# Two message-passing layers on one core: the second layer sums its messages one unit later, makes its edge weights from halves of the partitions, and takes more rows by products

## The chip, the core and the metric

The kernel runs on one core of a Trainium2 chip. A core has five engines that run side by side, each with its own queue of instructions: TensorE (PE in the profile, with PEld for its weight loads), VectorE (DVE), ScalarE (ACT), GpSimd (POOL) and SyncE (SP), which here only starts transfers. The metric is the device time of one execution in microseconds (us). Three timed runs of the kernel before gave 5934.48, 5959.10 and 5971.08 us. One further execution was recorded by the profiler.

## The reference

There are 6250 nodes with 128 features and 200000 edges sorted by destination. Both layers normalise the node features, clip them at zero, send something along each edge, sum it at the destination and add the result to the features.

```python
h = relu(layernorm(x))
z = (h @ W).reshape(N, 8, 16)                       # layer 0: attention over edges
e = leaky_relu(el[src] + er[dst], 0.2)              # el, er: products of z with attn_l, attn_r
a = exp(e - segment_max(e, dst)[dst])
x = x + segment_sum(z[src] * a, dst) / segment_sum(a, dst) + bias

h = relu(layernorm(x))                              # layer 1: products of features and edge data
s, v = h[:, :32] @ W_up_s, einsum(h[:, 32:], W_up_v)
w0, w1, w2, w3 = split(silu(silu(edge8 @ A1 + b1) @ A2 + b2) @ A3, 4)     # weights of each edge
mji = concat(s[src]*y_s*w0, dot(v[src], y_v)/sqrt(3)*w3, s[src]*y_v*w1, v[src]*y_s*w2)
message = segment_sum(mji, dst) / 10
x = x + concat(ms @ W_out_s, mv @ W_out_v)
```

So each layer needs, for each of the 200000 edges, one row of a table of 6250 rows: the row of the edge's source node.

## The kernel before

Edges are laid out in 1563 tiles of 128 (one edge per partition), and 16 tiles make a block: `KB` = 16, `NB` = 98 blocks. Since edges are sorted by destination, a block touches a window of 128 nodes. Sums are made by TensorE: a tile of one-hot rows (`one_hot`, line 1170) times the tile of messages, accumulated over the block in one PSUM bank `p_u`.

**Rows by source.** A tile's 128 source rows are fetched in one of three ways.
- An indirect transfer issued by GpSimd (`gather`, line 836, issued in line 839): one instruction for each tile.
- Row by row from SyncE (`rows_by_row`, line 1141, issued in line 1154): 128 transfers of one row each, for the last tile of each third block.
- By products on TensorE, for tile `KD` = 14 of the blocks named in the sets `dense` (layer 0, line 1200) and `dense1` (layer 1, line 1201). The whole table lies in SBUF as three bf16 parts (`t0s`, `t1s`), a one-hot matrix of the sources is made by VectorE (`ends_to`, `dense_ends`), and 17 groups of 3 products pick the rows (`rows_of` line 1304, `dense_rows` line 1911).

The gathers of a block are issued in `take_rows`, three blocks ahead in layer 0 and two ahead in layer 1, into five buffers that go round.

**The start.** GpSimd gathers the raw features of the first `KX` = 25 tiles while the first table is being made (`gather_x`, line 903); those rows are normalised and multiplied like the table itself. The remaining tiles of block 1 come from the finished table `t0`. Five of the normalising steps of the table run on GpSimd (line 960). A count then decides between this path for evenly spread edges and a general one (line 1005); the profiled execution took this path.

**Layer 0** loops over blocks in an order written out by hand for TensorE, VectorE, ScalarE and SyncE. `asked` (line 1262) loads three tiles of the first table, `split` (line 1277) splits them into the bf16 parts, once per block.

**Between the layers** the last `NL` = 3 tiles of nodes aren't ready when the first gathers of layer 1 could start. The first `NE` = 24 tiles are gathered early, from a copy of the table `t1z` with zeros in those nodes, and what is missing is added by products (`late_ends`, `late_rows`).

**Layer 1** loops over units of four tiles (391 of them), in this order on TensorE: half a step of the edge network of the next block (`network`, line 1755, bank `p_h`, two of them), the edge weights of the next unit (`tensor_weights`, line 1780, two products of 256 columns over 128 partitions, for two tiles each; bank `p_w`, two of them), products for rows (`dense_step`), and the sums of this unit (`sums1`, line 1819, bank `p_u`, two of them), for which it waits for this unit's messages (`messages`, line 1794, on VectorE). A finished block is taken out by `finish` (line 1178), a finished tile of nodes is put out by `node1` (line 1831), whose bank is a part of `held`. `edge_rows` (line 1747) loads the edge data two blocks ahead.

Of the kernel before, what the change touches and what calls it, by code (L numbers as in the profile page):

```python
# [9 lines left out]
F32 = mybir.dt.float32  # L10
# [3 lines left out]
OP = mybir.AluOpType  # L14
# [4 lines left out]
P = 128  # L19
# [5 lines left out]
MU = 32  # L25
# [716 lines left out]
def tile_even_edges(  # L742
# [63 lines left out]
    KX = KB + 9  # L806
# [49 lines left out]
    with tc.manual_schedule(engines={mybir.EngineType.PE, mybir.EngineType.DVE,  # L856
# [81 lines left out]
        def rows_of(gx, xs, fp, fp_ps, raw=None):  # L938
# [5 lines left out]
            for k in range(NC + 3):  # L944
# [3 lines left out]
                if 0 <= c < NC:  # L948
# [3 lines left out]
                    for j in range(n):  # L952
# [4 lines left out]
                        else:  # L957
                            late = by in (0, 3, 5) and NC - 4 <= c < NC - 2 and not raw
                            eng = nc.gpsimd if late else nc.vector
                            eng.tensor_scalar(h[:, j, :], xs[c][:, j, :], mvs[c][:, j, 0:1],  # L960
                                              rs[:, j, :], op0=OP.subtract, op1=OP.mult)
# [49 lines left out]
def even_edges(tc, v):  # L1011
# [8 lines left out]
    with ExitStack() as ctx:  # L1020
# [28 lines left out]
        NL, NE = 3, 24  # L1049
# [83 lines left out]
        nc.sync.dma_start(a1p, v["a1p"])  # L1133
# [44 lines left out]
        def finish(b, p_u, width, carry, agg, pool):  # L1178
# [8 lines left out]
            carry = pool.tile([WB, MW], F32, name="carry")  # L1187
            nc.scalar.copy(carry[:, :width], p_u[WB:, :width])
            return carry, agg
# [10 lines left out]
        dense = set(range(-(-NX // TS) + 4, NB - 4))  # L1200
        dense1 = set(range(10, NB - 4, 4))
# [36 lines left out]
        with tc.manual_schedule(engines=in_order), \  # L1238
# [338 lines left out]
            for g in range(NG - 3):  # L1577
# [7 lines left out]
                asked(g - 2)  # L1585
# [29 lines left out]
                if was:  # L1615
                    rows_of(n1, half + 4, NR)
                if b4:
                    weights(b4)
# [4 lines left out]
                er_of(n1, 1)  # L1623
                turned(n1, 2)
# [9 lines left out]
                if to:  # L1634
                    rows_of(n2, 0, 3)
# [21 lines left out]
                split(g - 3)  # L1657
# [77 lines left out]
        with tc.manual_schedule(engines=in_order), \  # L1735
# [11 lines left out]
            def edge_rows(b):  # L1747
                if b < NB:
                    c = blk[b]
                    c["ft"] = l1.tile([P, P], F32, name="ft", bufs=4)  # L1750
                    nc.sync.dma_start(c["ft"], f8[:, b, :])
                    c["yb"] = l1.tile([P, KB, 4], F32, name="yb", bufs=4)
                    nc.sync.dma_start(c["yb"], y4[:, b * KB : (b + 1) * KB, :])

            def network(b, step):

# [10 lines left out]
                p_h = l1_ps.tile([P, 4, P], F32, name="p_h")  # L1767
# [12 lines left out]
            def tensor_weights(u):  # L1780
# [3 lines left out]
                w = u["w"] = l1_ps.tile([P, 4, 4, MU], F32, name="p_w")  # L1784
                for k in range(0, m, 2):
                    q, n = (k0 + k) // 2, min(2, m - k)
                    nc.tensor.matmul(w[:, k : k + n].rearrange("p k a u -> p (k a u)"),  # L1787
                                     c["h2"][q // 4][:, q % 4, :],
                                     a3p[:, :n].rearrange("p k f -> p (k f)"), start=True, stop=True)
# [29 lines left out]
            def sums1(u):  # L1819
                b, k0, m = u["b"], u["k0"], u["m"]  # L1820
                if k0 == 0:
                    blk[b]["p_u"] = l1_ps.tile([P, 512], F32, name="p_u")
# [342 lines left out]
```

## Time and profile before

| | |
|---|---|
| median of 3 timed runs | 5959.1 us |
| the profiled execution's own time | 3749.37 us |
| its span, first to last instruction | 3747.6 us |
| what lies around the span | 1.8 us |
| granted TensorE clock, mean | 0.936 |
| busy: PE, DVE, ACT, POOL | 85%, 70%, 38%, 75% |
| gathers in the span (1750 + 589 + 583 from tables, 24 from `t1z`, 25 raw) | 2971 |
| row transfers by SyncE | 7808 |

The profiled execution is 2209.7 us shorter than the median of the timed runs. The profile shows one execution only, and nothing in it tells where the timed runs spend the difference. "Busy" counts the time in which an engine has an instruction in it; TensorE's records overlap and their ends are modelled, so the start-to-start distance of its groups tells its pace better. Starting a transfer on SyncE isn't counted as busy.

### The profile page before, as it was taken

Reading aid. Unit: us, or ns where it says so; the run is one execution under the profiler, and the core shown is the slowest. Engines: PE = TensorE matmul, PEld = TensorE weight load, DVE = VectorE, ACT = ScalarE, POOL = GpSimd, SP = SyncE. Lnnn points to the kernel's source line nnn. Section 1 sums busy time; section 2 is a strip of 40 time slices with the busy share of each in tenths; the row PEclk is TensorE's granted clock in tenths of the full one; section 3 lists DMA queues with packets and bytes.
Section 4 is the critical chain, followed back from the end, with each engine's and each line's share of the span. In section 5 each row is a group of like instructions: output and inputs, shape, how many; then the busy total and the mean of one; then the engine's idle time right before and its main releaser. Section 6 shows DMA issues by size and latency. Waiting matters only on the chain. (4 is left out here: it accounts for less than half of the span.)

```text
span 3747.6 us, 74803 instructions
## 1 busy us (share of the span) xinstructions
PE 3196.4 (85%) x19845; PEld 2474.1 (66%) x19845; DVE 2633.1 (70%) x6272; ACT 1406.0 (38%) x3638; POOL 2817.3 (75%) x2981
## 2 busy tenths in 40 slices
PE   4756788888888888888788899999999999999997
PEld 4655566666666666666666677777677777767775
DVE  7755666666666666666657777777777777777776
ACT  4432333333333333333334444444444444444443
POOL 7777777777777777777777777777777777777776
PEclk7766899999999999999799999999999999999999
DMA  6333332222222222222223222222222222222222
GB/s 167 75 78 79 71 68 67 68 69 68 68 68 68 68 68 67 69 69 67 71 70 95 69 64 64 64 64 64 64 64 64 65 63 64 65 63 64 63 68 52
DMA packets 212534, 262.78 MB, mean 70 GB/s; under 512 B 77425, under 2 KB 163921, under 8 KB 212097
## 3 DMA queue, kind: packets, MB, share of 16 engines
q0 software_dynamic: 95072, 200.78, 22.6%
q1 hardware_dynamic: 116592, 57.03, 5.7%
q8 instruction: 159, 2.61, 0.3%
q14 instruction: 279, 2.28, 0.2%
q10 hardware_dynamic: 432, 0.09, 0.0%
HBM read 236.19 MB, written 21.14 MB: 69 GB/s over the span
## 5 line engine op out<-in xcount | busy, mean ns | idle before, releaser
L839 POOL DMA_INDIRECT fz<-ft,fsrc x1750 | 1654.1, 945 | 539.5 <-issue 327.0
L1824 PE MATMUL p_u<-mj,s 128*128 128x256 f32 x3126 | 764.3, 388 | 87.5 <-DVE mj L1816 86.5
L1313 PE MATMUL p_x<-t0s,fz_first 128*128 128x408 bf16 (+1 forms) x3723 | 730.0, 346 | 0.0
L1824 PEld LDWEIGHTS p_u<-mj,s 128*128 128x128 f32 x3126 | 582.2, 192 | 215.6 <-DVE mj L1816 139.7
L839 POOL DMA_INDIRECT fz_other<-ft,fsrc x589 | 557.2, 946 | 179.6 <-issue 107.6
L839 POOL DMA_INDIRECT fz_second<-ft,fsrc x583 | 554.0, 950 | 178.3 <-issue 107.9
L1313 PEld LDWEIGHTS <-fz_first 128*128 128x128 bf16 x3723 | 361.5, 101 | 231.5 <-issue 17.4
L1791 ACT ACTIVATE p_w<-p_w,yb 128x64 f32<-128x64 f32 x1563 | 451.5, 289 | 117.3 <-PE p_w L1787 73.8
L1787 PE MATMUL p_w<-fa3p,h 128*128 128x256 f32 x1564 | 408.4, 384 | 0.0
L1787 PEld LDWEIGHTS p_w<-fa3p,h 128*128 128x128 f32 x1564 | 286.7, 193 | 114.5 <-issue 48.8
L1772 ACT ACTIVATE h<-p_h,fb 128x512 f32<-128x512 f32 x196 | 134.7, 687 | 585.8 <-PE p_h L1770 575.1
L1337 ACT COPY mk<-p_m 128x384 f32<-128x384 f32 (+1 forms) x99 | 47.4, 479 | 658.5 <-PE p_m L1333 651.6
L1427 PE MATMUL p_u<-fz,s 128*128 128x136 f32 x1846 | 272.9, 308 | 20.1 <-DVE fz L1422 20.1
L1427 PEld LDWEIGHTS p_u<-fz,s 128*128 128x128 f32 x1846 | 258.5, 216 | 23.8 <-DVE fz L1422 22.2
L1173 DVE TENSOR_TENSOR s<-p_i,fdloc 128x512 f32<-128x512 f32 x391 | 268.6, 687 | 3.8 <-ACT p_i L1766 3.8
L1173 DVE TENSOR_TENSOR s<-p_m,fdloc 128x512 f32<-128x512 f32 x391 | 266.2, 682 | 3.0 <-ACT mk L1337 2.7
L1770 PE MATMUL p_h<-ft,fa1p 128*128 128x128 f32 x1568 | 216.1, 282 | 56.5 <-DMA ft<-in_e_f_dram 56.3
L1770 PEld LDWEIGHTS p_h<-ft,fa1p 128*128 128x128 f32 x1568 | 208.7, 197 | 79.8 <-issue 55.7
L1348 ACT CAST d<-p_d 128x512 bf16<-128x512 f32 x391 | 229.3, 586 | 78.0 <-PE p_d L1346 34.2
L1378 DVE TENSOR_TENSOR_SCAN pe<-mk,pe 128x128 f32<-128x128 f32 x98 | 42.0, 428 | 290.8 <-PE pe L1293 271.6
L1777 ACT ACTIVATE h<-p_h,fb 128x512 f32<-128x512 f32 x196 | 134.7, 687 | 260.4 <-PE p_h L1774 260.4
L1811 DVE TENSOR_REDUCE vd<-vy 128x128 f32<-128x384 f32 x391 | 229.6, 587 | 0.0
(285 smaller groups left out, 4880.5 us busy)
## 6 DMA issues: line engine op xcount, KB each, us to landing
r<-ft SPq DMA_DIRECT2D x3968, 0.5 KB
r<-ft SPq DMA_DIRECT2D x3840, 0.5 KB
fz<-ft,fsrc POOLq DMA_INDIRECT x1750
fz_other<-ft,fsrc POOLq DMA_INDIRECT x589
fz_second<-ft,fsrc POOLq DMA_INDIRECT x583
fx<-x SPq DMA_DIRECT2D x47, 160.0 KB
ft<-in_e_f_dram SPq DMA_DIRECT2D x98, 64.0 KB
t1s<-fx SPq DMA_DIRECT2D x7, 576.0 KB
```

The lines of the kernel that those rows point to most:

```text
L839: nc.gpsimd.indirect_dma_start(out=to[:, k, :width], out_offset=None, in_=table, in_offset=bass.IndirectOffsetOnAxis(ap=src_col[:, t : t + ...
L1173: nc.vector.tensor_tensor(s[:, :m], iota[:, None, :].to_broadcast([P, m, P]), dloc[:, t : t + m].unsqueeze(2).to_broadcast([P, m, P]), OP. ...
L1313: nc.tensor.matmul(c["p_x"][:, :m, :], c["oh", k // half][:, k % half, :], t0s[:, i::NR, s, :], start=k == 0 and s == 0, stop=k == NR - 1 ...
L1348: nc.scalar.copy(d[:, :m], p_d[:, :m])
L1427: nc.tensor.matmul(c["p_u"][:, :ZW], c["s"][k // 4][:, k % 4, :], c["z"][:, k, :], start=c["o"] + k == 0, stop=c["o"] + k == KT[c["b"]] - 1)
L1770: nc.tensor.matmul(p_h[:, q, :], a1p[:, q0 + q, :], c["ft"], start=True, stop=True)
L1772: nc.scalar.activation(c["h1"], p_h, AF.Silu, bias=b1)
L1777: nc.scalar.activation(h2, p_h, AF.Silu, bias=b2)
L1787: nc.tensor.matmul(w[:, k : k + n].rearrange("p k a u -> p (k a u)"), c["h2"][q // 4][:, q % 4, :], a3p[:, :n].rearrange("p k f -> p (k f) ...
L1791: nc.scalar.activation(w[:, k, ::2, :], w[:, k, ::2, :], AF.Copy, scale=c["yb"][:, k0 + k, 0:1])
L1811: nc.vector.tensor_reduce(vd, vy.rearrange("p t i u -> p t u i"), AX.X, OP.add)
L1824: nc.tensor.matmul(blk[b]["p_u"][:, :MW], u["s"][:, k, :], u["mj"][:, k, :], start=k0 + k == 0, stop=k0 + k == KT[b] - 1)
```

## The change

- In the start, `KX` grows from 25 to 29, and the five normalising steps on GpSimd go to VectorE.
- In layer 0, `dense` begins with block 12 and not 21; `asked` and `split` are called twice per block, for numbers 2g - 4 and 2g - 3 in block g, and not once for g - 2 and g - 3. `rows_of`, `turned` and `er_of` move within the step of a block.
- Between the layers, `NE` grows from 24 to 28.
- In layer 1, `dense1` takes three of eight blocks and not one of four. Counted out, that is 32 blocks for 21; in layer 0 it is 82 for 73.
- `sums1` runs one unit later, after the next unit's weights, and `finish` with the copy of the carry after that (`block_ended`).
- `tensor_weights` makes each tile's weights by its own product of 128 columns over 64 partitions, low and high half in turn, in another order of `a1p`; `p_w` takes two banks for each of its two buffers.
- `p_h` and `p_u` have one bank each for two; `node1` and `late_ends` use the bank of the network.
- `edge_rows` runs three blocks ahead with five buffers; the very last unit is cut in two.

```diff
-    KX = KB + 9
+    KX = KB + 13
...
-                            late = by in (0, 3, 5) and NC - 4 <= c < NC - 2 and not raw
-                            eng = nc.gpsimd if late else nc.vector
-                            eng.tensor_scalar(h[:, j, :], xs[c][:, j, :], mvs[c][:, j, 0:1],
-                                              rs[:, j, :], op0=OP.subtract, op1=OP.mult)
+                            nc.vector.tensor_scalar(h[:, j, :], xs[c][:, j, :], mvs[c][:, j, 0:1],
+                                                    rs[:, j, :], op0=OP.subtract, op1=OP.mult)
...
-        NL, NE = 3, 24
+        NL, NE = 3, 28
...
-        nc.sync.dma_start(a1p, v["a1p"])
+        halves = [a.rearrange("p (u k) (q f) -> p u k q f", k=2, q=2) for a in (a1p, v["a1p"])]
+        for k in range(2):
+            for q in range(2):
+                nc.sync.dma_start(halves[0][:, :, q, k, :], halves[1][:, :, k, q, :])
...
-        dense = set(range(-(-NX // TS) + 4, NB - 4))
-        dense1 = set(range(10, NB - 4, 4))
+        dense = set(range(-(-NX // TS // 2) + 3, NB - 4))
+        dense1 = {b for b in range(10, NB - 4) if b % 8 in (2, 4, 7)}
...
-                asked(g - 2)
+                for k in range(2):
+                    asked(2 * g - 4 + k)
...
-                split(g - 3)
+                for k in range(2):
+                    split(2 * g - 4 + k)
...
-                p_h = l1_ps.tile([P, 4, P], F32, name="p_h")
+                p_h = l1_ps.tile([P, 4, P], F32, name="p_h", bufs=1)
...
-                w = u["w"] = l1_ps.tile([P, 4, 4, MU], F32, name="p_w")
-                for k in range(0, m, 2):
-                    q, n = (k0 + k) // 2, min(2, m - k)
-                    nc.tensor.matmul(w[:, k : k + n].rearrange("p k a u -> p (k a u)"),
-                                     c["h2"][q // 4][:, q % 4, :],
-                                     a3p[:, :n].rearrange("p k f -> p (k f)"), start=True, stop=True)
+                p_w = l1_ps.tile([P, 4, 2 * P], F32, name="p_w")
+                w = u["w"] = p_w[:, :, :P].rearrange("p k (a u) -> p k a u", u=MU)
+                for t in sorted(range(k0, k0 + m), key=lambda t: t % 2):
+                    q, half_t = t // 4 * 2 + t % 2, t // 2 % 2
+                    on = slice(64 * half_t, 64 * half_t + 64)
+                    nc.tensor.matmul(p_w[:, t - k0, :P], c["h2"][q // 4][on, q % 4, :], a3p[on, half_t],
+                                     start=True, stop=True)
...
-                    blk[b]["p_u"] = l1_ps.tile([P, 512], F32, name="p_u")
+                    blk[b]["p_u"] = l1_ps.tile([P, 512], F32, name="p_u", bufs=1)
...
+                p_n = l1_ps.tile([P, 4, P], F32, name="p_h", bufs=1)[:, :2]
...
+            def block_ended():
+                nonlocal carry, agg, ends
+                if ends is not None:
+                    p_u, to_carry = blk[ends]["p_u"], l1n.tile([WB, MW], F32, name="carry")
+                    nc.scalar.copy(to_carry, p_u[WB:, :MW])
+                    agg = finish(ends, p_u, MW, carry, agg, l1n)
+                    carry = to_carry
+                    if ends % 2 == 1:
+                        done.append((ends // 2, agg))
+                    ends = None
...
                 late_ends(4 * (i + 2))
+                if i:
+                    ends = sums1(us[i - 1])
                 messages(u)
...
-                sums1(u)
-                if k0 + m == KT[b]:
-                    ends = b
```

## The prediction

> **What bounds the kernel now.** I read the page's first part, then the busy times by stage, then GpSimd's timeline, then TensorE's within one unit. In the first line TensorE looks like the bound.
>
> ```profile
> PE 3196.4 (85%) x19845; PEld 2474.1 (66%) x19845; DVE 2633.1 (70%) x6272; ACT 1406.0 (38%) x3638; POOL 2817.3 (75%) x2981
> ```
>
> The stages speak otherwise. One stretch of layer 0, one of layer 1 (columns: length, then PE, PEld, DVE, ACT, POOL with counts, clock, DMA):
>
> ```profile
> 1499.20:1686.60 187.40, 165.97 (x1297) 122.35 (x1295) 126.71 (x265) 58.46 (x134) 141.91 (x150) 0.95 0.30 69
> 3185.80:3373.20 187.40, 170.83 (x842) 132.32 (x843) 141.21 (x349) 81.62 (x229) 141.66 (x151) 0.99 0.25 64
> ```
>
> The layers differ in work, but GpSimd issues 150 or 151 gathers in both. Its timeline (start, length, idle before in brackets) says why:
>
> ```profile
> 3005.59 0.94 POOL L839 DMA_INDIRECT fz<-ft,fsrc  x1 [0.30 <-issue]
> 3006.84 0.95 POOL L839 DMA_INDIRECT fz<-ft,fsrc  x1 [0.30 <-issue]
> ...
> 1869.61 0.94 POOL L839 DMA_INDIRECT fz<-ft1z,fsrc  x1 [0.31 <-issue]
> 1876.60 0.94 POOL L839 DMA_INDIRECT fz<-ft,fsrc  x1 [6.04 <-PE p_h L1868]
> ```
>
> A gather starts each 1.248 us, whatever else runs: 0.94 in it and a fixed 0.30 before the next. The only long gap is 6.04 us between the layers. So GpSimd's "75% busy" is a full engine: 2971 gathers x 1.248 = 3708 us of a span of 3747.6. Every buffer is free in time, so all others keep up. How closely TensorE does is seen in one unit of layer 1:
>
> ```profile
> 2999.75 1.05 PE L1770 MATMUL p_h<-ft,fa1p 128*128 128x128 f32 x8
> 3000.64 1.03 PE L1787 MATMUL p_w<-fa3p,h 128*128 128x256 f32 x4
> 3001.51 1.63 PE L1917 MATMUL p_x<-t1s,ohs 128*128 128x384 bf16 x9
> 3002.97 1.89 PE L1824 MATMUL p_u<-mj,s 128*128 128x256 f32 x8
> 3004.70 1.02 PE L1774 MATMUL p_h<-h,fa2p 128*128 128x512 f32 x2
> ```
>
> From start to start: network 0.89 (0.85 for its other half), weights 0.87, nine row products 1.46, sums 1.73. A block of four units costs 4 x (0.87 + 0.87 + 1.73) = 13.9 us, a block with row products 51 x 0.162 + 0.2 = 8.5 more, and `node1` 0.7 (1.39 each second block). With one block in four that is 13.9 + 2.1 + 0.7 = 16.7 us; GpSimd needs (16 - 1/3 - 1/4) x 1.248 = 19.2.
>
> **The change, part by part**, against the profiled execution's own 3749.4 us.
>
> *Fewer gathers.* Layer 0: 82 blocks for 73, layer 1: 32 for 21, so 20 gathers go, on the path: 20 x 1.248 = 25.0 us. In their place stand products on TensorE and one-hot rows on VectorE. In layer 0 blocks 21 to 93 ran so already, with the gather at its pace; the nine new blocks are the same. In layer 1 TensorE rises to 13.9 + 3.2 + 0.7 = 17.8 per block, GpSimd falls to 15.29 x 1.248 = 19.08. The cover thins from 2.5 to 1.3 us per block, 0.32 per unit. VectorE has 25% free.
>
> *Start.* The five steps on GpSimd (4.21 us, with 0.46 and 0.16 idle around them) become five of 0.28 on VectorE, whose work at that place ends with the count for the branch at 37.3 us, while GpSimd reaches the branch at 40.4. GpSimd would now reach it at 22.9 + 13 x 1.25 + 0.3 = 39.5, VectorE's count is done at about 38.7. Gain 4.5 us, at least 3 if the table's last rows land late. A rule speaks against it: the Trainium skill (SBUF — State Buffer, section Who interferes with whom) has such a one-input VectorE step able to take the port pair shared with GpSimd for its whole length, which would add up to 5 x 0.28 = 1.4 us to gathers. In the trace four such steps at 20.98 lie over the gather at 21.44, which took 0.95 like all others. I take 0. Four more raw gathers replace four from the table: no change in number. Their rows cost VectorE, ScalarE and TensorE some 3 us before layer 0, where gathers, at 20 us a block, are awaited.
>
> *Between the layers.* The table is complete 37.1 us after layer 0's last gather (1839.49 to 1876.60). 24 gathers fill 30.0 of that, 28 fill 34.9: 5.0 us gained, none lost. `late_ends` for four more tiles has three VectorE steps of 0.74, and holds the one `p_h`; at most 2.2 us per unit for seven units, and buffers hold two blocks of gathers, 38 us. Nothing reaches GpSimd.
>
> *Weights by halves.* Two products of 256 columns become four of 128: the same columns streamed, 0.87 us per unit. The skill (TensorEngine Tiling, Theoretical Speedup) lets two 64-row halves run side by side: down to 0.43. Its Key Properties say against it that changing the tiling mode drains TensorE, twice per unit. The trace has no such switch in a stream; the nearest row is a 128x128 product that shows 0.27 us alone and 0.11 in a stream of half-products, so a drain exposes some 0.16, two 0.32. By the first rule the step saves 0.43, by the second it costs 0.32, by both 0.1 is saved. I take -0.1 per unit: TensorE's block is 17.4, still under 19.08. Both ends, -0.43 and +0.32, leave GpSimd the bound, the last one just.
>
> *Sums a unit later.* TensorE's 86.5 us of waiting for messages (108 times) mostly goes; what comes late next in layer 1 is still the gather. The new waits: with one `p_u`, a block's first sums wait for `finish` on VectorE, behind messages and one-hot rows; TensorE's network and weights stand ahead of it, dense products, `node1` and the next unit behind it: up to 1 us per block, within the cover. With one `p_h` a network step waits for ScalarE's 0.69 us of the step before, ended a unit earlier: 0; `node1` waits for the same 0.69, with weights and sums ahead of it.
>
> *SyncE.* A row takes 0.385 us, 42.7 per block, 16.4, and its other transfers about 1.4: 17.8 of 19.1 us. The four pieces of `a1p` add three issues of about 0.45 once. `asked` at twice the rate waits on `split` for its two buffers; behind it stand the row and node transfers, which have five blocks of lead. Edge data a block earlier ends TensorE's 56.3 us of waiting for it, off the path. 0 from all.
>
> *End.* The last unit in two pieces, one step later: 1 us either way, taken as 0.
>
> Sum: 25.0 + 4.5 + 5.0 = 34.5, so 3749.4 becomes 3714.9, down 0.9%.
>
> **To the timed runs.** They took 5959.1, and 2209.7 us of that are in no profile row. If they lie outside what is edited, 34.5 remain: 5924.6. If they lie on the gathers, each costs 5959.1 / 3749.4 of the pace, or 1.248 + 2209.7 / 2971 = 1.99 us: 20 x 1.99 = 39.8, 4.5 at the start, and nothing between the layers, as 24 x 1.99 = 47.8 us already exceed 37.1. That is 44.3: 5914.8. As GpSimd is the one engine with no slack, I take the latter: **5915 us**, -0.7%.
>
> **Rivals.**
>
> *Something else paces the timed runs, and the edits don't reach it.* The page's own time is 37% below them, so the bound there may be SyncE (7808 row transfers, unchanged: 0.385 + 0.28 us each would give 5959), or time that no edit touches, or a path of the program not seen here. For it: the size of the gap. Against it: nothing in the trace hints at a wait of that kind. Gain 0 to 10: 5955.
>
> *TensorE becomes the bound of layer 1: slower.* The place is the weights step, the price the two changes of tiling mode in each of 391 units. It decides from 0.32 us per unit. At 0.3 per change without the halves overlapping, the cost is (0.6 - 0.32) x 391 = 110 us, less the 34.5: 3825 in the profile's measure, 6035 in the timed one. If TensorE is what is stretched in the timed runs (x1.59), the 20 blocks of row products cost 20 x 8.5 x 1.59 = 270 on top of whatever the halves bring: up to 6200. For it: 91% busy in layer 1. Against it: its records overlap, and its start-to-start sum is 16.7 of 19.2.
>
> *More than the sum.* If the timed runs stretch everything alike (x1.59), 34.5 becomes 55: 5904; with waits for edge data and messages counting there too, 5880.
>
> **How the numbers follow.** My forecast 0.55, the unreached bound 0.18, TensorE 0.15, more 0.12. A measurement of this kernel tells about 1% from no change: the three runs spread over 0.6%. Faster by over 1% (below 5899.5) is most of the last rival and the lower edge of the forecast: 0.20. Slower by over 1% (above 6018.7) is most of TensorE's case and a strange one: 0.18. Within 1%: 0.62. The range, 5885 to 6000, leaves out the upper half of TensorE's case and the lower of the last.
>
> **What would show it.** Right: 2951 gathers still 1.248 us apart, a gap near 1 us between the layers, the first table gather at about 40.3, a span near 3713. Wrong: gathers in layer 1 released by VectorE or TensorE with idle over 0.3 us; weights steps over 1.2 us from start to start; a profile shorter by 34 us beside timed runs that don't move, which would say that the timed runs aren't paced by gathers.

## The result, and the profile after

The change makes the kernel slower: 6178.3 us (median of 4, 6162.9 to 6189.7) against 5951.9 us (median of 4, 5934.5 to 5971.1), a ratio of 1.038, 95% interval 1.034 to 1.042. The forecast was 5915, within 5885 to 6000: 0.7% faster, where the kernel is 3.8% slower.

One thing has to be known to read the numbers: the kernel before takes about 3750 us in some executions (the first kind below) and about 5900 us in others (the second kind), the profile that the prediction was made from is of the first kind and all the times it was to explain are of the second, and every ratio here is between runs of one kind.

The profile after is of the second kind: its execution took 6179.1 us with a span of 6177.4. The engines' busy times come first, then the clock granted to TensorE in 40 equal slices, in tenths of full speed:

```profile
PE 4050.1 (66%) x22511; PEld 2783.1 (45%) x22511; DVE 2696.1 (44%) x6401; ACT 1391.4 (23%) x3643; POOL 2790.7 (45%) x2956
...
PEclk7667777777777777777766788888888888888889
```

No engine is full any more. GpSimd, which the prediction called full at 75%, is at 45% with nearly as many microseconds of work. Two stretches as long as those of the prediction, one in layer 0 and one in layer 1 (columns: length, PE, PEld, DVE, ACT, POOL with counts, clock, DMA), show 88 and 100 gathers in place of 150 and 151:

```profile
1499.20:1686.60 187.40, 124.52 (x744) 78.75 (x744) 70.09 (x146) 32.46 (x74) 83.07 (x88) 0.76 0.17 40
4500.00:4687.40 187.40, 141.95 (x702) 95.69 (x701) 93.69 (x234) 50.63 (x145) 93.71 (x100) 0.84 0.16 42
```

Who waits for whom in after (waiting engine and what it writes, what it waited for, total us, times, longest):

```profile
ACT mk L1337 <- remote: 1090.3, 58, 24.2
DVE pe L1378 <- remote: 978.1, 60, 19.9
PEld L1313 <- issue: 865.8, 1470, 2.7
POOL fz L839 <- PE p_u L1427: 707.7, 107, 16.8
POOL fz L839 <- DVE mj L1821: 614.5, 102, 49.1
DVE agg L1188 <- ACT carry L1987: 581.7, 75, 12.8
...
PE p_u L1829 <- DVE agg L1188: 132.3, 38, 5.4
```

The gathers wait for buffers, in both layers, and the other engines wait for something that the profile can't name ("remote", "issue"). One row of gathers in the timeline of after, all engines together, shows how the two belong together:

```profile
1577.97 0.68 PE L1313 MATMUL p_x<-t0s,fz_first 128*128 128x408 bf16 x3
1578.60 0.94 POOL L839 DMA_INDIRECT fz<-ft,fsrc  x1 [0.30 <-issue]
1579.02 0.33 PE L1313 MATMUL p_x<-t0s,fz_first 128*128 128x408 bf16 x1 [0.36 <-issue]
...
1581.10 0.95 POOL L839 DMA_INDIRECT fz<-ft,fsrc  x1 [0.30 <-issue]
1581.14 0.33 PE L1313 MATMUL p_x<-t0s,fz_first 128*128 128x408 bf16 x1 [1.06 <-issue]
...
1586.84 0.50 PE L1313 MATMUL p_x<-t0s,fz_first 128*128 128x408 bf16 x1 [1.64 <-issue]
1587.78 0.94 POOL L839 DMA_INDIRECT fz<-ft,fsrc  x1 [0.75 <-remote]
1588.93 0.50 PE L1313 MATMUL p_x<-t0s,fz_first 128*128 128x408 bf16 x1 [1.59 <-issue]
...
1591.22 0.43 DVE L1378 TENSOR_TENSOR_SCAN pe<-mk,pe 128x128 f32<-128x128 f32 x1 [18.25 <-remote]
1591.25 0.48 ACT L1337 COPY mk<-p_m 128x384 f32<-128x384 f32 x1 [20.85 <-remote]
...
1593.33 3.94 PE L1313 MATMUL p_x<-t0s,fz_first 128*128 128x408 bf16 x12
```

While gathers follow one another at their usual 1.25 us, TensorE's row products, 0.17 us apart in a stream at full clock, come one at a time with up to 1.64 us between them and no wait that the profile can name. VectorE and ScalarE, whose inputs TensorE wrote by 1577.9, stand still for 18 and 21 us. All of them start again at 1591.2, 3.4 us after the start of the last gather. Behind the pause the clock is low: twelve products take 3.94 us, 0.33 each, and the granted clock (the last column but two) is half:

```profile
1583.20:1596.80 13.60, 8.20 (x32) 4.40 (x32) 4.01 (x8) 2.06 (x6) 3.86 (x5) 0.50 0.12 26
```

Below I call this slow issue. I count it in the traces of SyncE's instructions and TensorE's weight loads: at least four steps of 0.70 us or a multiple of it from start to start, less than 1.5 us apart, make a stretch. The profile of before that the prediction used has none. The one of after has 201, together 2426 us, and between its gathers lie 2402 us beyond their pace of 1.25 us each, where that profile of before had some 20.

### The profile page after: what moved, and what is told of

It is laid out like the page before. It is cut to its first block, busy times and chain, and to the rows that moved or that the text cites. A ratio compares the mean times of both kernels' runs of the same rounds, so it can differ in the third digit from the quotient of the medians.

```text
span 6177.4 us, 80263 instructions
## 1 busy us (share of the span) xinstructions
PE 4050.1 (66%) x22511; PEld 2783.1 (45%) x22511; DVE 2696.1 (44%) x6401; ACT 1391.4 (23%) x3643; POOL 2790.7 (45%) x2956
## 5 line engine op out<-in xcount | busy, mean ns | idle before, releaser
L1313 PE MATMUL p_x<-t0s,fz_first 128*128 128x408 bf16 (+1 forms) x4182 | 1119.3, 403 | 514.1 <-issue 512.4
L1829 PE MATMUL p_u<-mj,s 128*128 128x256 f32 x3126 | 908.1, 436 | 197.6 <-DVE agg L1188 132.3
L1313 PEld LDWEIGHTS <-fz_first 128*128 128x128 bf16 x4182 | 458.3, 113 | 1002.1 <-issue 865.8
L1829 PEld LDWEIGHTS p_u<-mj,s 128*128 128x128 f32 x3126 | 637.3, 215 | 355.2 <-DVE agg L1188 140.1
L1924 PE MATMUL p_x<-t1s,ohs 128*128 128x384 bf16 (+1 forms) x1632 | 329.6, 344 | 91.9 <-issue 73.6
L1777 PE MATMUL p_h<-h,fa2p 128*128 128x512 f32 x392 | 268.8, 774 | 170.5 <-ACT h L1775 135.7
L1775 ACT ACTIVATE h<-p_h,fb 128x512 f32<-128x512 f32 x196 | 134.7, 687 | 996.0 <-remote 441.0
L1793 PEld LDWEIGHTS p_w<-fa3p,h 64*128 64x128 f32 x3126 | 241.6, 214 | 236.5 <-issue 146.3
L1793 PE MATMUL p_w<-fa3p,h 64*128 64x128 f32 x3126 | 326.6, 331 | 14.8 <-issue 9.6
L1188 DVE TENSOR_TENSOR agg<-p_u,carry 64x256 f32<-64x256 f32 x96 | 40.0, 417 | 630.7 <-ACT carry L1987 581.7
L1924 PEld LDWEIGHTS <-ohs 128*128 128x128 bf16 x1632 | 165.4, 102 | 233.7 <-issue 129.0
```

What stands on the lines that cost most here:

```text
L1313: nc.tensor.matmul(c["p_x"][:, :m, :], c["oh", k // half][:, k % half, :], t0s[:, i::NR, s, :], start=k == 0 and s == 0, stop=k == NR - 1 ...
L1775: nc.scalar.activation(c["h1"], p_h, AF.Silu, bias=b1)
L1777: nc.tensor.matmul(p_h.rearrange("p q e -> p (q e)"), a2p, c["h1"].rearrange("p q e -> p (q e)"), start=True, stop=True)
L1793: nc.tensor.matmul(p_w[:, t - k0, :P], c["h2"][q // 4][on, q % 4, :], a3p[on, half_t], start=True, stop=True)
L1829: nc.tensor.matmul(blk[b]["p_u"][:, :MW], u["s"][:, k, :], u["mj"][:, k, :], start=k0 + k == 0, stop=k0 + k == KT[b] - 1)
L1924: nc.tensor.matmul(c["p_x"][:, :m, :], c["oh"][:, k, :], t1s[:, i::NR, s, :], start=k == 0 and s == 0, stop=k == NR - 1 and s == 2)
```

## The experiments

Four theories stood at the start. A: each 16,384-byte piece of TensorE's code costs 13.8 us (2203 us of difference over 159 pieces; after has 179 pieces, and 20 x 13.8 less the 34.5 of the prediction gives +241, near the +226 measured). B: TensorE's own time is stretched. C: each gather costs 1.99 us, as the prediction assumed. D: the new waits in layer 1 cost it. E came out of the second set: rows of gathers and the other engines' work exclude each other. (A row is a run of gathers that follow one another without a wait.)

**First set, beside before at 3744.1.** `before_again` is before unchanged. `a_wide` is after with the edge weights as they were:

```
-                p_w = l1_ps.tile([P, 4, 2 * P], F32, name="p_w")
...
-                for t in sorted(range(k0, k0 + m), key=lambda t: t % 2):
...
+                w = u["w"] = l1_ps.tile([P, 4, 4, MU], F32, name="p_w")
+                for k in range(0, m, 2):
...
```

`b_filler` and `b_bigfill` add to `masks_of` of before, ahead of its product, 26 tiny products or 8 large ones:

```
+                for _ in range(26):
+                    nc.tensor.matmul(p_m[:1, :1], identb[:, :1], identb[:, :1], start=True, stop=True)
```

```
+                for _ in range(8):
+                    nc.tensor.matmul(p_m[:kr, :MC], rsel[:, j, o * H : o * H + kr], masks[:, g, :], start=True, stop=True)
```

> The kernel before, unchanged, profiled once more. Theory A (the time of every 16,384-byte piece of TensorE code is what the timed runs pay for): if the profiled execution takes about 5950 us, it holds 159 pieces on the instruction queue, and after a piece stretches in which TensorE issues one instruction each 0.71 us whatever its size, as the trace of after has them; GpSimd's gathers still start each 1.248 us where they come in a row, and wait for TensorE or VectorE between rows. Layer 0 then ends near 3200 us. Theory B (TensorE runs all its products about 1.6 times as long): the pace of twelve row products rises from 2.07 to about 3.3 us everywhere, with no such stretches. Theory C (each gather costs 1.99 us): gathers start each 1.99 us with no wait for another engine. If the execution is again of about 3750 us, none of this can be seen.

> The kernel after, with the edge weights again by two products of 256 columns for four tiles instead of four of 128 by halves. Theory A: 1562 products fewer in the trace's count, with their weight loads 3124 TensorE instructions or 12.2 pieces of code; at 13.8 us each (2203 us beyond the fast profile of before, over its 159 pieces) the time falls by 168 us to 6010. Theory B (the time follows TensorE's busy time): the columns are the same, the halves' switch of tile costs at most 0.3 us in each of 391 units: 6060 to 6180, and if halves run side by side more than after. Theory C (gathers at 1.99 us each): 6178. Theory D (the waits of layer 1's single banks p_h and p_u and the sums a unit later make the loss): 6178, as they stay.

> The kernel before, with 26 products of one column by one, each with its weight load, put ahead of the mask product of each of 99 blocks of layer 0; their sum is overwritten by the mask product. Theory A: 5148 more TensorE instructions are 20.1 pieces; x 13.8 = 277, so 6229. Theory B: such a product of few columns takes 0.03 to 0.06 us from start to start; 99 x 26 x 0.04 = 103 us of TensorE's time, x 1.59 = 164 at most, less what is hidden: 5952 to 6116. Theory C: no gather is touched: 5952. Theory D: nothing in layer 1 is touched: 5952.

> The kernel before, with the mask product of each of 99 blocks of layer 0 repeated eight times more (128 x 384 bf16, 0.16 us each in a stream). TensorE's time is more than with the 26 small products: 99 x 8 x 0.16 = 127 us; its instructions are 1584, or 6.2 pieces. Theory A: 6.2 x 13.8 = 85, so 6037, under a third of what the small products cost. Theory B: 127 x 1.59 = 201, so up to 6153, more than the small ones. Theories C and D: 5952.

Measured: before_again 3753.7, a_wide 3745.5 (ratio 1.000, 0.999 to 1.001), b_filler 3756.1 (1.003, 1.002 to 1.004), b_bigfill 3817.1 (1.019, 1.018 to 1.021). No profile of this set has slow issue, so A could not be tested here: the 26 small products per block, 20 more pieces of code (179 for 159), cost 12 us in this kind. What the set does show is the prediction's own sum in its own kind of execution. a_wide has all of the change but the halves (after itself was never run in this kind), and the 34.5 us forecast did not come. GpSimd's timeline of a_wide, first within layer 0, then between the layers, says where they went:

```profile
1541.47 0.94 POOL L839 DMA_INDIRECT fz<-ft,fsrc  x1 [2.13 <-PE p_u L1424]
...
1839.74 0.95 POOL L839 DMA_INDIRECT fz<-ft,fsrc  x1 [0.31 <-issue]
1850.16 0.95 POOL L839 DMA_INDIRECT fz_first<-ft1z,fsrc  x1 [9.47 <-DMA ft1z<-sv]
...
1891.15 0.95 POOL L839 DMA_INDIRECT fz<-ft,fsrc  x1 [6.03 <-PE p_h L1871]
```

The first gather of the next layer now waits 9.47 us for its table; the wait behind the 28 gathers is still 6.03, where before had 6.04 behind its 24. And layer 0's last gather starts at 1839.7 as in before (1839.5), though nine gathers fewer lie ahead of it: from 1316 us on, eleven gathers wait for their buffer until TensorE's sums (`p_u` of layer 0) have read it, 12 us beyond the pace, as much as the nine had saved. So in layer 0 TensorE was no longer hidden, and the whole table of layer 1 came 14.5 us later (1891.15 for 1876.60). Behind it the rest of the sum came nearly as forecast: from there to the end a_wide takes 17.4 us less, where 15 gathers fewer make 18.7. Which edit of layer 0 holds TensorE up in this kind was not tried.

**Second set, beside before at 5903.8.** after once more, and before with `dense = set()` and `dense1 = set()`, so that every block gathers all its tiles.

> The kernel after, unchanged, once more beside before: the chip of the last runs ran before in 3744 us, without the stretches of slow issue, while the first comparison of before and after was made where before took 5952. If before is near 3744 here: theory A (the loss comes from the number of pieces of TensorE code, which cost 13.8 us each only where code comes in slowly) expects no loss of 3.8%, but 3715 by the sum of the prediction, or 3745 as with the wide weights; theories B, C and D (TensorE's own time, the gathers' pace, the waits of layer 1) are tied to no such condition: D expects the same 3.8%, 3886. If before is near 5950: 6178 by every theory, and the profile of a second execution of it shows which engine the gathers wait for.

> The kernel before with all gathers issued: no block of either layer takes its first tile's rows by products on TensorE instead (94 gathers more; 94 x 51 products and as many weight loads fewer: 9682 TensorE instructions or 37.8 pieces of code). If before is near 3744: the gathers bound it, 94 x 1.248 = 117 us more, 3861, by theories A and C; less if TensorE bounds part of it. If before is near 5950: A: 37.8 x 13.8 = 522 less, and 117 more at most for the gathers: 5430 to 5550. B: 94 blocks x 8.5 us x 1.59 = 1270 us of TensorE's time less, of which as much is saved as TensorE is the bound: 4700 to 5950. C: 94 x 1.99 = 187 more, 6139.

Measured: after_again 6131.6 (1.039, 1.036 to 1.042), the same loss as at first; b_nodense 5789.6 (0.981, 0.978 to 0.984). So 94 more gathers and 39 pieces of TensorE code less (120 for 159) save 114 us: C has the wrong sign, and A asked for some 400. Its trace, with the least work on TensorE of all, has more slow issue than after (2837 us): SyncE slows down and VectorE and ScalarE stand still while a row of gathers runs, whether TensorE has products to issue or not. That became E.

**Third set, beside before at 5898.1.** before profiled in this condition; `a_olddense`, after with the two sets of before; `a_plain`, this with the wide weights too; and `b_halfgather`, which is before without the gathers of odd tiles from block 8 of each layer on (1376 of 2971 left out; those tiles are computed from rows that an earlier block left in the buffer):

```
                                            and not (c["b"] in dense and k % KB == KD)
+                                           and (c["b"] < 8 or k % 2 == 0)], ZW)
...
                                                 and not (b in dense1 and k % KB == KD)
+                                                and (b < 8 or k % 2 == 0)], P)
```

> The kernel before, profiled once more, for the case that this chip runs it in about 5900 us. Theory E, from the traces of after and of the kernel without row products there: from 1.5 to 6.5 us after the first gather of a row until about 3.5 us after the start of its last, TensorE, SyncE, VectorE and ScalarE together issue one instruction each 0.70 us, and only GpSimd's gathers go on; so the gathers and the other engines' work follow one another instead of running side by side. It then shows some 200 such stretches of some 2500 us together, and blocks of layer 0 of some 33 us with row products and 30 without. Theory A (each piece of TensorE code costs 13.8 us): such stretches only behind the 159 pieces. If before is near 3744: none of this.

> The kernel after, with row products in the blocks of before (73 in layer 0, 21 in layer 1): 2060 TensorE instructions fewer and 20 gathers more than after. Chip with before near 5904, where after takes 6132: theory A: 8.05 pieces x 13.8 less 25: 6046. Theory E: a block with row products took 33.3 us in layer 0 where one without took 30.0, so 9 x 3.3 = 30 less there, and up to 11 x (8.5 - 1.25) = 80 less in layer 1: 6022 to 6102. Theory D (layer 1's single banks and later sums): 6120. Chip with before near 3744: 3750 to 3770, as 20 gathers more are 25 us.

> The kernel after with both the wide weights and the row products of before: what is left of the change are the sums a unit later with their single banks, the start, 28 gathers between the layers, and the order in layer 0. TensorE's instructions are those of before to within 25. Chip with before near 5904: theory A: before less some 10: 5895. Theory D: the loss is all here: 6090 to 6130. Theory E says nothing of the waits itself: what a_plain has over before is the price of the waits, what after has over a_plain that of row products and halves. Chip with before near 3744: 3735 by the sum of the prediction (start and between the layers), up to 3770 if the waits cost.

> The kernel before, from block 8 of each layer on without the gathers of odd tiles (some 1376 of 2971 left out): those tiles are computed from the rows that stand in the buffer from an earlier block. All other instructions stay. Chip with before near 5904: theory E: each gather's 1.25 us comes off as long as it is not hidden: 5904 - 1376 x 1.25 = 4184, more if the stretches don't reach their beginning in rows of eight, down to the 3300 us that TensorE needs. Theory A: the pieces of code are the same: 5904. Theory C (1.99 us a gather): 5904 - 1376 x 1.99 = 3166, bounded by TensorE's 3300. Chip with before near 3744: TensorE's 16.7 us a block is the bound: 3300 by theories C and E.

Measured: before_slow 5907.2; a_olddense 6113.5 (1.037, 1.033 to 1.041); a_plain 6053.8 (1.026, 1.022 to 1.030); b_halfgather 4167.1 (0.707, 0.704 to 0.709). b_halfgather settles A: its TensorE code is that of before, 159 pieces, and it takes 1731 us less. That it comes within 17 us of E's 4184 is in part luck: E took off 1.25 us for each gather, while in the trace slow issue falls from 2491 to 351 us. before_slow's first line and its two stretches:

```profile
PE 3733.4 (63%) x19845; PEld 2722.2 (46%) x19845; DVE 2630.8 (45%) x6272; ACT 1392.6 (24%) x3638; POOL 2822.1 (48%) x2981
```

```profile
1499.20:1686.60 187.40, 120.82 (x763) 80.85 (x764) 75.65 (x159) 35.20 (x80) 80.59 (x86) 0.77 0.16 39
4500.00:4687.40 187.40, 128.89 (x572) 96.68 (x571) 94.33 (x236) 51.79 (x148) 96.86 (x104) 0.87 0.16 43
```

This is the profile the prediction would have needed: 86 and 104 gathers in 187 us, not 150; slow issue for 2491 us in 204 stretches; 2095 us that GpSimd waits between gathers. It also refutes my wording of E in part. In the stretches SyncE goes at 0.70 us or a multiple all the time; TensorE joins only in some of them (about 75 of some 200) or some microseconds later. B does not stand either: where no slow issue falls in, TensorE's pace is that of the first profile (the weights of a unit 0.87 us from start to start in both), and the low clock goes with the pauses.

a_plain has TensorE's work of before and still loses 2.6%: most of the harm is in the start, the order and the later sums, not in the products. With the halves on top (a_olddense) it is 59.8 us more, some 35 either way. TensorE's weight loads for them (a_plain first, then a_olddense; at the end the idle time before them) wait longer for issue:

```profile
L1788 PEld LDWEIGHTS p_w<-fa3p,h 128*128 128x128 f32 x1564 | 336.4, 226 | 176.7 <-issue 123.7 <-DVE mj L1817 15.9 <-DVE vy L1808 2.0
```

```profile
L1793 PEld LDWEIGHTS p_w<-fa3p,h 64*128 64x128 f32 x3126 | 244.8, 217 | 242.9 <-issue 153.6 <-DVE agg L1188 22.5 <-DVE mj L1821 22.3
```

The products themselves are not slower. A unit of after outside slow issue:

```profile
5317.88 1.05 PE L1773 MATMUL p_h<-ft,fa1p 128*128 128x128 f32 x8
5318.86 0.72 PE L1793 MATMUL p_w<-fa3p,h 64*128 64x128 f32 x8
5319.51 1.99 PE L1829 MATMUL p_u<-mj,s 128*128 128x256 f32 x8
5321.34 1.63 PE L1924 MATMUL p_x<-t1s,ohs 128*128 128x384 bf16 x9
```

From start to start the weights take 0.65 us where the wide ones take 0.87, the network step ahead of them 0.98 for 0.89, the sums behind them 1.83 for 1.73 (medians over the trace agree). The halves do run side by side, and what they save is taken back by their neighbours: 0.02 us less per unit.

The three traces of this set, cut at the first mask copy on ScalarE and at the first gather of `ft1z`, say where it went (us; two traces of after differ by 60 us in the last part, 36 of them more than their sets differ, so small differences there say little):

| | start | layer 0 | rest | span |
|---|---|---|---|---|
| before_slow | 162.8 | 2917.7 | 2824.6 | 5905.1 |
| a_plain | 173.3 | 3000.3 | 2866.7 | 6040.4 |
| a_olddense | 172.5 | 3001.4 | 2928.7 | 6102.7 |

**Fourth set, beside before at 5943.3.** `a_oldorder` is a_plain with the steps of a block of layer 0 in the order of before:

```
-                er_of(n1, 1)
-                turned(n1, 2)
                 if b4:
                     weights(b4)
...
                 for n in nodes:
                     node_x(n)
-                if to:
-                    rows_of(n2, 0, 3)
+                er_of(n1, 1)
+                turned(n1, 2)
...
+                if to:
+                    rows_of(n2, 0, 3)
                 for n in nodes:
                     node_d(n)
```

`b_l0nodense` is before with `dense = set()`. `b_pause4` and `b_pause3` are before with rows of gathers broken up, behind each fourth or third:

```
+            if i and i % 4 == 0:
+                n = min(4, KB - k)
+                nc.gpsimd.tensor_copy(to[:1, k : k + n, :1], to[:1, k - 1 : k, :1].to_broadcast([1, n, 1]))
```

> As a_plain (wide weights, row products of before), and in layer 0 the steps of a block in the order of before: the second part of the er products and the third of the turned one-hots behind the nodes' rows, the next block's first row products behind the weighted rows. Chip with before near 5900, where a_plain took 6054 and its layer 0 ended 92 us later than that of before, its blocks of layer 1 took 0.58 us longer: if the order costs what layer 0 lost: 6054 - 92 = 5962. If the doubled pace of split and asked, or the start, costs it: 6054. If layer 1's waits are all: 6054, with layer 0 ending as before. Chip with before near 3744: 3735 to 3750.

> The kernel before, with no block of layer 0 taking its first tile's rows by products (73 gathers more), layer 1 as before. Chip with before near 5900: the kernel with no such block in either layer ended layer 0 118 us earlier than before, and its blocks of layer 1 took 0.12 us longer; so 5898 - 118 = 5780, the best of all. Chip with before near 3744: 73 x 1.248 = 91 more: 3835, less what TensorE's work in layer 0 held up.

> The kernel before, with a copy of one to four numbers on GpSimd behind each fourth gather of a block, which waits for that gather's landing; the places it writes are overwritten by the next gathers. Rows of gathers are four long (now and then eight), with some 1.7 us between them: 4 gathers in 3 x 1.25 + 3 = 6.8 us, a block in 26.6. Theory E (the row of gathers keeps the other engines to one instruction each 0.70 us, from the fourth gather on): chip with before near 5900: stretches fall from 2500 us to under 500, a block takes 26.6 us in both layers instead of 31.5 and 27.7: 5898 - 98 x (4.9 + 1.1) = 5310. If the stall has nothing to do with rows, pauses only add: over 5900. Chip with before near 3744: the gathers bound it, 26.6 for 18.7 a block: 5290, slower.

> As b_pause4 with rows of three: 3 gathers in 2 x 1.25 + 3 = 5.5 us, a block in 28.7. Theory E: hardly a stretch of slow issue left, but the pauses cost more: 5898 - 98 x (2.8 - 1.0) = 5720, between b_pause4 and before. If the row has nothing to do with it: over 5900, more than b_pause4. Chip with before near 3744: 5700.

Measured: a_oldorder 6038.7 (1.015, 1.011 to 1.019), b_l0nodense 5869.0 (0.987, 0.984 to 0.991), b_pause4 5161.2 (0.868, 0.865 to 0.871), b_pause3 5435.4 (0.914, 0.911 to 0.918). The order in layer 0 alone is worth 1.1 of the 3.8 points (0.6 either way), and a_oldorder's layer 0 takes 2941.8 us, which in a set where before is 0.77% longer is before's 2917.7. b_l0nodense saves 74 us (1.3%) where 118 (2.0%) were expected. And adding copies and waits to GpSimd takes 13% off before. b_pause4 more than halves slow issue, to 1048 us. Some of its rows are joined to seven or eight, and most of the rest lies in these. The sizes were missed: b_pause4 was expected at 5310 with under 500 us of slow issue, b_pause3 at 5720.

**Last sets, beside before at 5909.7, and at 5954.2 for the last kernel.** `a_banks` is a_oldorder without `bufs=1` on p_h and p_u in layer 1 (the wide weights leave room); `a_pause4` is after with the edit of b_pause4. `b_rest` holds rows to four from one buffer to the next too, with a copy that waits for the third gather's landing and eight settings behind it; `b_rest0` is without the settings:

```
+            if i % 4 == 0 and len(recent) > 1:
+                n = min(4, KB - k)
+                of, j = recent[-2]
+                nc.gpsimd.tensor_copy(to[:1, k : k + n, :1], of[:1, j : j + 1, :1].to_broadcast([1, n, 1]))
+                for _ in range(8):
+                    nc.gpsimd.memset(to[:1, k : k + n, :1], 0.0)
+            recent.append((to, k))
```

> As a_oldorder, with two banks each for p_h and p_u in layer 1 (the wide weights leave the room); the sums stay a unit later. Chip with before near 5900, a_oldorder at 1.0148 of it: if the single banks cost the rest: 1.000 to 1.003 of before. If the later sums, or what lies ahead of layer 0, cost it: 1.015 as a_oldorder. Chip with before near 3744: 3735 to 3745 in both cases.

> The kernel after, with the same copy on GpSimd behind each fourth gather of a block as in b_pause4. Chip with before near 5900 (b_pause4 was at 0.868 of before): theory E: where the rows are broken up, the other engines' work is hidden again and 20 gathers fewer count as in the prediction: 20 x 1.248, and five pauses of some 2.1, some 35 us less than b_pause4: 0.862 of before. If the loss of the change comes from TensorE's added work or layer 1's waits whatever the gathers do, the 3.8% stay: 0.90. Half of each, as rows of seven and eight are still left: 0.88. Chip with before near 3744: 5100.

> The kernel before with rows of four gathers everywhere, also from one buffer to the next, and a shorter rest between them: a copy that waits for the landing of the row's third gather, and eight settings of four numbers on GpSimd; what they write is overwritten by the gathers. 4 gathers in about 6.3 us, a block in 24.5. b_pause4 still had 145 rows of seven or eight and 1050 us of slow issue. Theory E: with rows of four only, slow issue falls under 300 us, and a block takes the gathers' 24.5: about 5050 where before takes 5900. If GpSimd's settings hold up the others as its gathers do, or the rest is too short: as before or worse, 5300 to 5900. Chip with before near 3744: 4950.

> As b_rest (before with rows of four gathers everywhere), without the eight settings: the rest is the copy alone, which waits for the landing of the row's third gather; some 2.2 us from gather to gather there instead of 3.5. A row of four takes 3 x 1.25 + 2.2 = 5.9 us, a block 23.1. Chip with before near 5900: theory E, if this rest is enough: slow issue under 300 us, 98 x 2 x 23.1 + 180 = 4710, or 4900 where TensorE begins to hold. If the rest has to be longer: stretches of slow issue over 1000 us, 5160 or more. Chip with before near 3744: the gathers' pace bounds it, 4700.

Measured: a_banks 6001.4 (1.018, 1.014 to 1.022), a_pause4 5162.5 (0.875, 0.872 to 0.877), b_rest 5621.8 (0.952, 0.949 to 0.954), b_rest0 5148.5 (0.865, 0.863 to 0.868). The single banks are not it: with two banks TensorE's wait for `agg` (150.6 us in a_oldorder) is gone from the trace, 156.2 us of waiting for VectorE's messages `mj` stand in its place, and the time is no better. Cut like the table above and scaled to the same before, a_oldorder is some 12 us behind before_slow where layer 0 begins, 14 where it ends and 94 at the end; a_banks 13, 11 and 69. So most of what is left of the loss there lies behind layer 0. With rows broken up, after stands 0.8% above before (0.8745 / 0.8677 = 1.008, some 0.5 points either way) where it was 3.8% above: most of the loss hangs on the rows, but the gain I expected of a_pause4 did not come. In b_rest slow issue is all but gone, and the rests have become the bound, as GpSimd's timeline shows:

```profile
2300.51 0.18 POOL L844 COPY fz_other<-fz_other 1x4 f32<-1x4 f32 x1 [0.46 <-DMA fz_other<-ft,fsrc]
2300.76 1.17 POOL L846 MEMSET fz_other<- 1x4 f32 x8
2302.56 0.98 POOL L848 DMA_INDIRECT fz_other<-ft,fsrc  x1 [0.63 <-POOL fz_other L846]
2303.84 1.05 POOL L848 DMA_INDIRECT fz_other<-ft,fsrc  x1 [0.30 <-issue]
```

From the last gather at 2299.10 to the next at 2302.56 are 3.46 us, a row of four takes 7.2, a block of layer 0 28.3 and not the 24.5 expected. b_rest0 was expected at 4710 to 4900 if its rest was long enough, and it was not. Slow issue and time of the kernels, by the length of their rows of gathers (a row ends where a gather starts more than 1.6 us after the one before):

| | rows of gathers | slow issue, us (stretches) | us |
|---|---|---|---|
| before, profile of the prediction | as they come | 0 | 3749 |
| before_slow | to 16 | 2491 (204) | 5907 |
| b_nodense | to 16 | 2837 (217) | 5790 |
| b_halfgather | mostly 2 to 8 | 351 (34) | 4167 |
| b_pause4 | 4, joined to 8 | 1048 (165) | 5161 |
| b_rest0 | 4, rest 2.1 | 656 (142) | 5148 |
| b_rest | 4, rest 3.5 | 66 (21) | 5622 |

The count depends on how near to 0.70 us a step has to lie: between 0.02 and 0.04 us before_slow moves by 4%, b_rest0 by almost half. And the time does not follow slow issue alone, as the rests cost too.

## Why the prediction was wrong, point by point

**The step that failed** is the one from the profile to the timed runs: "As GpSimd is the one engine with no slack, I take the latter", which put the 2209.7 us that no row showed on the gathers, 1.99 us each, and kept all else hidden under them. In the timed kind of execution a gather keeps its pace (median 1.25 us in before_slow and in after), and GpSimd has the slack that it lacks in the profile: it waits 2095 of 5905 us. The missing time lies in the turns that the gathers and the other engines take: slow issue holds 2491 us of before_slow and none of the first profile, and breaking up the rows of gathers takes 13% off. With that the bound changes, and terms that were called hidden come into the sum. In points of before they are: order in layer 0 1.1, halves 1.1, new row products 0.2, all else 1.5 (a_oldorder), each uncertain by some 0.5. With the rows broken up, all of them together come to 0.8 (a_pause4).

The sum failed in the first kind too, where GpSimd is the bound: 34.5 us were forecast and a_wide gained none, because TensorE held up the gathers of layer 0, and layer 1's table came later.

- *Fewer gathers*, -25.0 (-39.8 by 1.99): the gathers do go, but in the second kind row products cost more than they save. 94 blocks of them cost 114 us net (b_nodense), 1.2 per block, so 24 for the 20 new ones by estimate; after_again over a_olddense gives 0.2 points, within their intervals. In the first kind the 11 gathers of layer 1 came off as forecast, and "the nine new blocks are the same" of layer 0 did not hold, whatever edit of layer 0 is to blame.
- *Start*, -4.5: layer 0's first mask copy comes 10 us later in a_plain and a_olddense than in before_slow. In a_wide the first table gather comes at 43.2 us, in the two profiles of before of that kind at 41.2 and 43.4, so nothing there either.
- *Between the layers*, -5.0: in a_wide the first of the 28 gathers waits 9.47 us for its table, and the wait behind them stays at 6.03; none were gained.
- *Weights by halves*, -0.1 per unit and off the path: the size on TensorE was about right, -0.02, and both rules I weighed hold in the trace: the halves run side by side (0.65 for 0.87) and the change of tile costs, some 0.1 on each side, which is less than my 0.16. What failed is "off the path": +59.8 us in the second kind, or 0.15 for each of 391 units. That the cost is the 3126 added TensorE instructions meeting slow issue is argued from the waits for issue (153.6 after 123.7), not isolated, and these 30 us are half of it.
- *The order in layer 0*: no term was given to it beyond `asked` and SyncE. Layer 0 takes 83 us longer in a_plain than in before_slow, and a_oldorder wins this back; by the times the order is 1.1 points, some 65 us. It was missing rather than mis-sized.
- *Sums a unit later*, "up to 1 us per block, within the cover": TensorE waits 132.3 us for `agg`, 1.4 per block, but without this wait a_banks gains nothing: VectorE is late either way. VectorE itself waits 581.7 us for ScalarE's copy of `carry` (691.0 in a_banks), a wait that I had not named, with the messages queued behind it. Of a_oldorder's 1.5 points the start is some 12 us, and most of the others fall behind layer 0. That the wait for `carry` makes them is argued and not shown; no kernel took the later sums alone back.
- *SyncE*, 0: it is slowed most regularly of all, but no kernel here changed its rows, so its part was not tried.

Of the rivals, "Something else paces the timed runs" was right in its first half, for the bound there is not the gathers' pace, and wrong in its second: the edits do reach it. "TensorE is what is stretched in the timed runs, up to 6200" gave nearly the right time by luck, for the wrong reason: the 20 blocks were to cost 270 us and cost, by estimate, some 24. The signs of being wrong that I listed came true: gathers of layer 1 released by VectorE with long idle times (614.5 us for one tile) are what the waits of after show.

**A version that beats both.** b_rest0 and b_pause4 take 13% off before where before takes 5900 us. Where it takes 3744 they were not run; there the gathers are the bound, and by the estimates given with them they would take some 4700 and 5290. So this is a gain for the second kind alone.

## What to carry to other kernels

Before anything is predicted from a profile, its own time has to be that of the timed runs; a gap of 37% is not to be spread over the rows of the profile, for what bounds the timed runs may be something else. What is hidden is hidden only under a cover that can run beside it: here long rows of gathers held up the engines that were to work under them, so steps "within the cover" had their price. Where one engine's row of instructions shuts out the others, shorter rows with rests between can be worth more than the work saved: here 13% against a loss of 3.8%.

## What the runs showed of the hardware that I had not expected

- The same program ran in 3753.7 us in one set and 5907.2 us in another, with the same instructions. What makes the difference is not known from these runs.
- In the second kind, from mostly 1.5 to 8 us after a row of gathers begins until about 3.5 us after the start of its last, SyncE, and in part of the cases TensorE, issue slowly, in steps of 0.70 us or a multiple; VectorE and ScalarE stand still for 18 and 21 us in the row shown. In before_slow about 190 of 200 rows of six gathers or more had such a stretch; in b_halfgather one at most of 395 rows of two or three. Rows of four depend on the rest between them: 142 stretches over 637 such rows with rests of 2.1 us (b_rest0), 21 with rests of 3.5 (b_rest). The transfers themselves are as quick as in the other kind: a gather's last piece starts 1.95 us after the gather in before_slow, 1.98 in the profile of before. Instruction supply is a natural suspect, since even SyncE's register moves take such a step. The traces speak against one form of it: TensorE's 159 pieces of code come in as quickly as in the first profile (median 1.02 us against 1.11), and more than half of the stretches of before_slow (119 of some 200) have no piece of any engine land in them. No run tells what is left of it from other causes.
- The pauses cost clock as well. The granted clock was 0.77 in layer 0 of before_slow and 0.95 in that of the first profile, and a row product took 0.33 us from start to start behind a pause against 0.17. In the row of after shown above it was 0.50 from 1583.2 to 1596.8 us and 1.0 on both sides. The Trainium skill (TensorE: Matmul & The Clock Gate, What's actually happening) has the clock halved after an idle window of some 3.4 us and full again after as long a busy one; the twelve products of 3.94 us agree with its half rate, and full speed is back 3.5 us after they begin. Idle did not mean without work: in the 3.4 us ahead of the drop TensorE had three products of 0.33 us.
